# Attention scores of a masked graph network: 4 matmuls of 32x128 or 16 matmuls of 32x32 per key tile

## The chip, the cores and the metric

The kernel runs on one core of a Trainium2 chip. The metric is the device time of one execution in microseconds. Before the change it was 3508.07 us, the median of three runs (3501.76 to 3508.48).

## The reference

Two layers work on x of 16 batches x 1024 nodes x 256 features, with a 0/1 adjacency matrix of 1024 x 1024 per batch. Each layer takes `h = relu(layernorm(x))` and adds its result to x. The change lies in the first layer, which is masked self-attention of 8 heads of 32 features, followed by an MLP:

```python
normed = layer_norm(h, gamma1, beta1)
qkv = normed.reshape(b, n, 8, 32).transpose(0, 2, 1, 3)
scores = einsum('bhqd,bhkd->bhqk', qkv, qkv) / sqrt(32)
attn = softmax(where(adj > 0, scores, -inf), axis=-1)
out = einsum('bhqk,bhkd->bhqd', attn, qkv)
x1 = h + out
layer0 = x1 + gelu(layer_norm(x1, gamma2, beta2) @ W1 + b1) @ W2 + b2
```

Queries, keys and values are the same array. The second layer is a graph attention of one head with weights `leaky_relu(Ax^T + Ay + h a_12 h^T)`, masked by the same adjacency, softmax, a product with the features, two projections and an `elu`. All arithmetic on TensorE is in f32, apart from the masks of batch 0, which are fp8.

## The kernel before

Two paths are in the program. A bound on gamma and beta chooses the fast one, `fast_path`, which is the only one that runs here; everything below is about it.

**Tiling of the first layer's attention.** The 1024 nodes are 8 tiles of 128 (`P`). Queries go in two halves of 512 (`QW`), heads in two groups of 4 (`GH`, `NG`). `kT[r, g, :]` holds the transposed normed features: partitions are the 4 x 32 features of the 4 heads of group `g`, so head `j` lies in partitions 32j to 32j+31 (`r`). For each unit (query half, head group, key tile), `scores` in line 950 makes, for each of the 4 heads, the product of 128 keys (the stationary operand, 32 partitions x 128 columns) and 512 queries (the moving operand, 32 partitions x 512 columns). The result of a head is 128 x 512 f32 in PSUM, one bank. The four heads use four row strips of the array, and each its own bank: heads 0 and 1 write `sc[0]`, heads 2 and 3 `sc[1]`, two buffers of one slot each (pool `psc`, `bufs=1`).

VectorE then adds the mask to a buffer of two heads (line 971), ScalarE takes the exponential (line 974), and in the turn after it `weigh` multiplies by the values (line 987): per head a matmul with 128 rows x 32 columns of stationary operand, the four heads in four column strips of the array, into the four partition quarters of one accumulator `o`. In batch 0 the mask of the first two heads is added by TensorE ahead of the scores, with an fp8 identity as stationary operand (`by_pe`), and the scores accumulate on it. The exponentials of the eight key tiles are summed by DMAs that GpSimd issues (line 1011).

**Quarters.** All other large matmuls go through the helper `matmul` in line 565, which splits a 128-column stationary operand into four matmuls of 32 columns (line 570), one for each column strip, as long as `quarters[0]` holds. It is switched off when the attention of the last batch closes. Transposes use the whole array.

**Order.** The program is written as six generators, which are merged by due places: `stream_a` runs the attention of batch b, and `stream_b` at the same time the rest of batch b-1 (MLP, then the second layer), in pieces of about 1.75 us of TensorE work. So TensorE's instruction order is: a score unit of one key tile, line 987 for the unit before, some pieces of the other stream, the next score unit. There are 16 x 2 x 2 x 8 = 512 score units. Within an engine the order of the program is kept.

**Shapes on the array.** In records of the profile, "32*128" is the shape of the stationary operand (rows * columns). So TensorE meets 32*128 for scores, 128*32 for line 987 and the helper's quarters, 128*128 for transposes.

Of the kernel before, what the change touches and what calls it, by code (L numbers as in the profile page):

```python
# [16 lines left out]
P = 128  # L17
# [476 lines left out]
def fast_path(  # L494
# [28 lines left out]
    nc = tc.nc  # L523
    B, N, D = x.shape
    DFF = W1.shape[1]
    H, HD = 8, D // 8
# [38 lines left out]
    def matmul(out, lhsT, rhs, start=True, stop=True):  # L565
        if not quarters[0]:
            nc.tensor.matmul(out, lhsT, rhs, start=start, stop=stop)  # L567
            return
        for c in range(0, P, HD):
            nc.tensor.matmul(out[c : c + HD], lhsT[:, c : c + HD], rhs, start=start, stop=stop)  # L570
# [165 lines left out]
    def defer(us, f):  # L736
        deferred.append((clock[0] + us, len(deferred), f))

        return clock[0] + us
# [145 lines left out]
    def make_turns():  # L885
        room = 3 - open_sums[0] - bool(summed) if open_sums[0] else 100
        while turns and turns[0][0] <= room:
            n, f = turns.pop(0)
            room -= n
            f()  # L890
# [40 lines left out]
    def attention(b, st):  # L931
        va, kT = st["va"], st["kT"]


        def scores(qh, g, kt):
            qs = slice(qh * QW, (qh + 1) * QW)
            sc = [
                psc.tile([P, 2, QW], F32, tag=f"sc{i}", name=f"s_{b}_{g}_{qh}_{kt}_{i}") for i in range(2)
            ]

            by_pe = 2 if b == 0 else 0
            if by_pe:
                for j in range(by_pe):
                    matmul(
                        sc[j // 2][:, j % 2, :], ident8, st[qh][:, kt // 2, :, kt % 2], start=True, stop=False
                    )
                clock[0] += 0.45
            for j in range(GH):
                r = slice(j * HD, (j + 1) * HD)
                nc.tensor.matmul(  # L950
                    sc[j // 2][:, j % 2, :],
                    kT[r, g, kt * P : (kt + 1) * P],
                    kT[r, g, qs],
                    start=j >= by_pe,
                    stop=True,
                )
            mb = st[qh][:, kt // 2, :, kt % 2].unsqueeze(1).to_broadcast([P, 2, QW])
            es = []
            if b == 0 and kt % 2:

                odd = midp.tile([P, 2, 2, QW], F32, tag="mid", name=f"odd_{g}_{qh}_{kt}")
            for i in range(2):
                if b == 0 and kt % 2:
                    e = odd[:, i]
                elif kt == 0:
                    e = accp.tile([P, 2, QW], F32, tag=f"acc{i}", name=f"acc_{b}_{g}_{qh}_{i}")
                else:
                    e = ep.tile([P, 2, QW], F32, tag="e", name=f"e_{b}_{g}_{qh}_{kt}_{i}")
                masked = sc[i]
                if 2 * i >= by_pe:  # L970
                    nc.vector.tensor_tensor(e, masked, mb, op=ALU.add)  # L971
                    masked = e
                es.append(e)
                weights = lambda e=e, masked=masked: nc.scalar.activation(e, masked, AF.Exp, scale=SCALE)  # L974
                if i == 0:
                    weights()
            return es, weights

        acc = {}


        def weigh(qh, g, kt, es):
            if kt == 0:
                acc[g, qh] = pso.tile([P, QW], F32, tag="o", name=f"o_{b}_{g}_{qh}")
            o = acc[g, qh]
            for j in range(GH):
                nc.tensor.matmul(  # L987
                    o[j * HD : (j + 1) * HD, :],
                    va[:, kt, (g * GH + j) * HD : (g * GH + j + 1) * HD],
                    es[j // 2][:, j % 2, :],  # L990
                    start=(kt == 0),
                    stop=(kt == NT - 1),
                )
            if b == 0 and kt % 2:

                if kt > 1:
                    for n, (e, w) in enumerate(zip(es, odds[g, qh])):
                        defer(1.0 + 2.5 * n, lambda e=e, w=w: nc.vector.tensor_add(e, e, w))
                odds[g, qh] = es
            if kt == NT - 1:  # L1000
                c = tmpp.tile([P, QW], F32, tag="w2", bufs=3, name=f"os_{b}_{g}_{qh}")
                nc.vector.tensor_copy(c, o)
                weighed.append((b, qh, g, c, [s[g, qh] for s in (sums, odds) if s]))

        sums, odds = {}, {}


        def add_up(qh, g, kt, e, i):
            if b == 0 and kt % 2:
                return  # L1010
            nc.gpsimd.dma_start(sums[g, qh][i], e, accum_op=ALU.add)  # L1011

        units = [(qh, g, kt) for qh in range(NQH) for g in range(NG) for kt in range(NT)]
        for u in units:
            make_turns()
            es, rest_of_weights = scores(*u)
            go_on()
            rest_of_weights()
            qh, g, kt = u
            if kt == 0:  # L1020
                sums[g, qh] = es
            else:
                for i in range(2):
                    defer(2.0 + 1.5 * i, lambda u=u, e=es[i], i=i: add_up(*u, e, i))
            scored.append((weigh, (*u, es)))
            yield

    def go_on():
        was_weighed, was_summed, was_totalled = weighed[:], summed[:], totalled[:]
        for l in (weighed, summed, totalled):  # L1030
            l.clear()
        if scored:
            f, args = scored.pop()
            f(*args)
        summed.extend(was_weighed)
        for args in was_summed:
            total(*args)
        for args in was_totalled:
            turns.append((2, lambda args=args: finish(*args)))
        clock[0] += 2.0  # L1040
# [501 lines left out]
```

## Time and profile before

| | before |
|---|---|
| median of 3 runs | 3508.07 us |
| the profiled execution | 3501.46 us |
| its span, first to last instruction | 3499.6 us |
| granted TensorE clock, mean | 0.998 |
| line 987, weights times values: busy, mean of one record | 461.8 us, 605 ns |
| line 971, masks added on VectorE: busy, mean | 1002.6 us, 1217 ns |
| line 974, exponentials on ScalarE: busy, mean | 896.0 us, 1057 ns |
| fillers of line 570, 256 columns: mean of one record | 379 ns |

How to read it. A line of the profile has the source line, engine, operation, the tiles written and read, the shape of the stationary operand, the moving operand and the count. Then come the busy time in us and the mean of one record in ns, then the engine's idle time ahead of them and what ended most of it. Busy time is the union of the records, so overlapping records count once. TensorE appears twice, as PE (matmuls) and as PEld (loads of the stationary operand). An f32 matmul is two LDWEIGHTS records and two MATMUL records, for two passes over the moving operand. The ends of matmul records are modelled, their starts are not, so distances between starts say more than durations.

### The profile page before, as it was taken

What the parts mean: (1) busy time and instruction counts of PE and PEld (TensorE: products, weight loads), DVE (VectorE), ACT (ScalarE), POOL (GpSimd) and SP (SyncE); (2) the same over time, 40 slices, a digit from 0 to 9 for tenths busy, and PEclk for the clock granted to TensorE, in tenths of its full rate; (3) what the DMA queues carried; (4) which work ended last, traced back from release to release, by engine and by line L of the source; (5) the groups of instructions that cost most, each with busy time, mean ns of one, the idle gap of its engine ahead of it and who ended that gap; (6) DMA issues with size and microseconds to landing.
All of it is one profiled execution on the core that took longest, in us unless ns stands there. A gap on an engine that the chain in (4) does not pass through costs nothing.

```text
span 3499.6 us, 107320 instructions
## 1 busy us (share of the span) xinstructions
PE 3445.0 (98%) x46590; PEld 1673.9 (48%) x46590; DVE 2758.3 (79%) x5193; ACT 1857.8 (53%) x2184; POOL 1412.8 (40%) x1708
## 2 busy tenths in 40 slices
PE   6999999999999999999999999999999999999998
PEld 2244444444444444444444444444444444444477
DVE  6878788787877878888787888878878777887754
ACT  4555555555555555555555555555555555555522
POOL 3444443434434344343444534344344443434220
PEclk9999999999999999999999999999999999999999
DMA  7798889999899998989989899998989989899720
GB/s 183 147 182 173 181 164 185 182 186 188 161 187 176 191 184 165 181 167 190 195 167 183 165 185 185 177 190 164 186 177 191 183 165 179 171 191 182 147 63 14
DMA packets 281860, 597.81 MB, mean 171 GB/s; under 512 B 94882, under 2 KB 130084, under 8 KB 281380
## 3 DMA queue, kind: packets, MB, share of 16 engines
q0 software_dynamic: 124416, 453.04, 70.1%
q1 hardware_dynamic: 154276, 134.41, 15.5%
q8 instruction: 368, 6.03, 0.7%
q10 hardware_dynamic: 2688, 3.41, 0.3%
q14 instruction: 112, 0.92, 0.1%
HBM read 104.21 MB, written 16.78 MB: 35 GB/s over the span
## 4 chain that ended last, share of the span: by engine, by line
PE 94%; DVE 3%; DMA 1%; issue 1%; ACT 0%; POOL 0%; ACTq 0%; SPq 0%; DVEq 0%; POOLq 0%
PE s L950 15%; PE o L987 13%; PE pa L570 12%; PE po L570 12%; PE ph L570 12%; PE lg L570 10%; PE pg L570 3%; PE pf L570 3%; PE puT L570 3%; PE den L901 2%; PE ptf L1193 1%; PE pty L1117 1%; PE ptk L801 1%; PE ptos L922 1%; PE pa L567 1%
## 5 line engine op out<-in xcount | busy, mean ns | idle before, releaser
L974 ACT ACTIVATE e<-e 128x1024 f32<-128x1024 f32 x852 | 896.0, 1057 | 964.3 <-DVE e L971 728.3
L1011 POOL DMA_DIRECT2D acc<-e x864 | 754.9, 890 | 1438.3 <-DMA acc<-e 637.3
L971 DVE TENSOR_TENSOR e<-s,mk 128x1024 f32<-128x1024 f32 x852 | 1002.6, 1217 | 181.2 <-PE s L950 155.4
L950 PE MATMUL s<-kT 32*128 32x512 f32 x4096 | 592.5, 643 | 3.5 <-DVE odd L971 2.7
L987 PE MATMUL o<-e,va 128*32 128x512 f32 x3456 | 461.8, 605 | 2.1 <-ACT e L974 2.1
L570 PE MATMUL pa<-gw,e 128*32 128x258 f32 x7648 | 453.0, 380 | 0.0
L570 PE MATMUL lg<-fT,uT 128*32 128x256 f32 x7680 | 447.3, 379 | 0.0
L570 PE MATMUL ph<-yT,w 128*32 128x256 f32 x7808 | 446.5, 379 | 0.0
L570 PE MATMUL po<-w,hid 128*32 128x256 f32 x7680 | 439.3, 379 | 0.0
L570 PEld LDWEIGHTS ph<-yT,w 128*32 128x32 f32 x7808 | 255.3, 110 | 211.8 <-issue 51.1
L570 PEld LDWEIGHTS po<-w,hid 128*32 128x32 f32 x7680 | 250.3, 110 | 208.8 <-issue 58.3
L570 PEld LDWEIGHTS pa<-gw,e 128*32 128x32 f32 x7648 | 248.4, 110 | 212.0 <-issue 56.5
L570 PEld LDWEIGHTS lg<-fT,uT 128*32 128x32 f32 x7680 | 249.6, 110 | 209.0 <-issue 43.4
L1241 DVE SCALAR_TENSOR_TENSOR e<-lg,gw,mk 128x256 f32<-128x256 f32 x512 | 223.2, 477 | 72.0 <-PE lg L570 61.5
L1247 ACT ACTIVATE e<-e,shift 128x512 f32<-128x512 f32 x256 | 183.1, 717 | 181.6 <-DVE e L1246 116.0
L1144 DVE TENSOR_TENSOR hid<-ph,b1c 128x512 f32<-128x512 f32 x256 | 175.8, 687 | 91.6 <-PE ph L570 80.1
L950 PEld LDWEIGHTS s<-kT 32*128 32x128 f32 x4096 | 162.7, 184 | 163.8 <-issue 112.0
L987 PEld LDWEIGHTS o<-e,va 128*32 128x32 f32 x3456 | 68.6, 108 | 330.3 <-issue 187.3
L974 ACT ACTIVATE acc<-acc 128x1024 f32<-128x1024 f32 x124 | 131.1, 1057 | 132.9 <-DVE acc L971 128.4
L1246 DVE SCALAR_TENSOR_TENSOR e<-e 128x512 f32<-128x512 f32 x256 | 193.1, 754 | 8.8
L971 DVE TENSOR_TENSOR acc<-s,mk 128x1024 f32<-128x1024 f32 x124 | 146.1, 1218 | 20.2 <-PE s L950 19.8
L793 POOL TENSOR_TENSOR nrm<-nrm,g 128x256 f32<-128x256 f32 x128 | 112.9, 882 | 63.8 <-DVE nrm L727 63.8
(145 smaller groups left out, 3820.9 us busy)
## 6 DMA issues: line engine op xcount, KB each, us to landing
acc<-e POOLq DMA_DIRECT2D x864, 512.0 KB, 6.1
adj<-in_adj_dram SPq DMA_DIRECT2D x248, 256.0 KB, 5.6
h<-in_x_dram SPq DMA_DIRECT2D x64, 256.0 KB, 6.1
xb<-in_x_dram SPq DMA_DIRECT2D x128, 128.0 KB, 4.3
out_dram<-z SPq DMA_DIRECT2D x128, 128.0 KB, 4.0
adj<-in_adj_dram SPq DMA_DIRECT2D x4, 512.0 KB, 6.8
mk<-mq SPq DMA_TRANSPOSE x128, 6.5
w<-in_L_gnn_W_dram ACTq DMA_DIRECT2D x2, 1024.0 KB
```

What stands on the lines that cost most here:

```text
L570: nc.tensor.matmul(out[c : c + HD], lhsT[:, c : c + HD], rhs, start=start, stop=stop)
L793: nc.gpsimd.tensor_mul(nrm, nrm, g1)
L901: nc.tensor.matmul(den[j * HD : (j + 1) * HD, :], ones, acc[j // 2][:, j % 2, :], start=acc is accs[0], stop=acc is accs[-1],)
L950: nc.tensor.matmul(sc[j // 2][:, j % 2, :], kT[r, g, kt * P : (kt + 1) * P], kT[r, g, qs], start=j >= by_pe, stop=True,)
L971: nc.vector.tensor_tensor(e, masked, mb, op=ALU.add)
L974: weights = lambda e=e, masked=masked: nc.scalar.activation(e, masked, AF.Exp, scale=SCALE)
L987: nc.tensor.matmul(o[j * HD : (j + 1) * HD, :], va[:, kt, (g * GH + j) * HD : (g * GH + j + 1) * HD], es[j // 2][:, j % 2, :], start=(kt = ...
L1011: nc.gpsimd.dma_start(sums[g, qh][i], e, accum_op=ALU.add)
L1144: nc.vector.tensor_tensor(hid[:, f0 : f0 + 2, :], ph, b1c[:, f0 : f0 + 2].unsqueeze(2).to_broadcast([P, 2, CW]), op=ALU.add,)
L1241: nc.vector.scalar_tensor_tensor(e[:, j, :], lg[:, j, :], gw[:, kt, D : D + 1], st[c // 2][:, kt // 2, qs, kt % 2], op0=ALU.add, op1=ALU.add,)
L1246: nc.vector.scalar_tensor_tensor(e, e, ALPHA, e, op0=ALU.mult, op1=ALU.max)
L1247: ready = defer(2.5, lambda: nc.scalar.activation(e, e, AF.Exp, bias=shift))
```

## The change

Each head's 128 keys are cut into four quarters of 32. A score matmul then has a stationary operand of 32 x 32 and writes 32 partitions of the head's bank; one unit has 16 of them, one for each combination of row strip (head) and column strip (key quarter). The order is head by head, and within a head quarter by quarter. The first matmul of a buffer in each quarter starts or continues the sum as before (`start=j >= by_pe`). Nothing else is touched.

```diff
             for j in range(GH):
                 r = slice(j * HD, (j + 1) * HD)
-                nc.tensor.matmul(
-                    sc[j // 2][:, j % 2, :],
-                    kT[r, g, kt * P : (kt + 1) * P],
-                    kT[r, g, qs],
-                    start=j >= by_pe,
-                    stop=True,
-                )
+                for c in range(0, P, HD):
+                    nc.tensor.matmul(
+                        sc[j // 2][c : c + HD, j % 2, :],
+                        kT[r, g, kt * P + c : kt * P + c + HD],
+                        kT[r, g, qs],
+                        start=j >= by_pe,
+                        stop=True,
+                    )
             mb = st[qh][:, kt // 2, :, kt % 2].unsqueeze(1).to_broadcast([P, 2, QW])
```

Lines after 950 stand one line lower in the changed kernel: its score matmuls are in line 951, weights times values in line 988.

## The prediction

> **What bounds the kernel now.** I read the page first, its parts 1 and 4, then the costliest groups, to learn which engine sets the end and what share of it the changed line holds.
>
> ```profile
> span 3499.6 us, 107320 instructions
> ...
> PE 3445.0 (98%) x46590; PEld 1673.9 (48%) x46590; DVE 2758.3 (79%) x5193; ACT 1857.8 (53%) x2184; POOL 1412.8 (40%) x1708
> ...
> PE 94%; DVE 3%; DMA 1%; issue 1%; ACT 0%; POOL 0%; ACTq 0%; SPq 0%; DVEq 0%; POOLq 0%
> ...
> L950 PE MATMUL s<-kT 32*128 32x512 f32 x4096 | 592.5, 643 | 3.5 <-DVE odd L971 2.7
> ```
>
> TensorE is busy in 98% of the span, and the chain that ended last runs through it for 94%. The changed line was kept waiting by others for 3.5 us in all. So the change is worth what it adds to or takes from TensorE's own time, 512 times: 16 batches x 2 query halves x 2 head groups x 8 key tiles. The 4096 records are 512 units of 8: each f32 matmul leaves two MATMUL records and two LDWEIGHTS records, two passes.
>
> Next the chain in order of time, for the cost of a unit on the path rather than its busy time, which holds modelled pipeline ends:
>
> ```profile
> 1999.85 0.87 PE pa L570 x16
> 2000.72 1.07 PE s L950 x8
> 2001.79 1.00 PE o L987 x8
> 2002.79 1.73 PE lg L570 x32
> ```
>
> One score unit holds the path for 1.07 us. Then the two lines' own instructions, with least, median and longest duration in ns:
>
> ```profile
> L950 PEld LDWEIGHTS s<-kT x4096: 181/184/333, 25.9 to 3334.7; 32*128 32x128 f32 x196
> L950 PE MATMUL s<-kT x4096: 587/692/1218, 25.9 to 3335.1; 32*128 32x512 f32 x196
> L987 PEld LDWEIGHTS o<-e,va x3456: 105/109/110, 43.3 to 3341.7; 128*32 128x32 f32 x192
> L987 PE MATMUL o<-e,va x3456: 592/593/618, 43.3 to 3342.1; 128*32 128x512 f32 x192
> ```
>
> A score's second pass lasts 587 and its first 692: 105 ns in which the first waits for its own 128 weight columns. In line 987, with 32 columns, the same difference is 618 - 592, some 26 ns. And last the timeline of TensorE in four slices of 4 to 7 ns at the start of one unit, then the one burst of tiny matmuls that the program has:
>
> ```profile
> 1988.13 0.69 PE L950 MATMUL s<-kT 32*128 32x512 f32 x1
> 1988.13 0.70 PE L950 MATMUL s<-kT 32*128 32x512 f32 x2
> 1988.13 0.71 PE L950 MATMUL s<-kT 32*128 32x512 f32 x3
> 1988.13 0.71 PE L950 MATMUL s<-kT 32*128 32x512 f32 x4
> ```
>
> ```profile
> 72.72 0.31 PE L570 MATMUL p_w_a<-a2c,stage 128*32 128x1 f32 x16 [0.65 <-ACT wm L689]
> 73.00 0.43 PE L570 MATMUL p_w_a<-a1c,stage 128*32 128x1 f32 x32
> ```
>
> The four heads of a unit start one after the other, 6.7 ns apart. The masks of batch 0 (fp8, one pass, two records per matmul) start 3.4 ns apart in the trace, so a tile's place in line costs 1.67 ns for each of its records, and four for an f32 matmul. A tile's second pass does not hold up the next tile: all four first passes start within 20 ns, the four second passes together 533 ns later. From the last second-pass start of a unit to the first weight load of line 987 are 516 ns in all 512 units.
>
> So the 1.07 us are: 105 (load of 128 columns, in the open) + 20 (three further starts) + 2 x 427 (two passes of 512 columns, as in 1.73 us for eight passes of 256) + 89 [...] = 1068.
>
> [...] 93 to 95 ns between the end of streaming and the first load at every change of shape, 88 to 89 when leaving 32x128, whichever shapes meet. [...]
>
> **The change, part by part.** Order on DVE, ACT, POOL and SP stays the same instruction for instruction, as do waits and DMAs. On TensorE, each of the 2048 score matmuls becomes four: 48 more records per unit, 24,576 in all, same arithmetic.
>
> *Removed:* the load of 128 columns becomes one of 32 in the open: 105 - 26 = 79 ns less[...]. 512 x 80 = 41.0 us less.
>
> *Added:* 16 starts in place of 4. Twelve more x 6.7 ns = 80 ns before the last tile begins; it still has its two passes to run, so its delay is the unit's. 512 x 80 = 41.0 us more. Bounds: [...] if the starts were wholly hidden, 0. Above, the sixteen f32 tiles need 64 records at once, and the densest 64 in this trace are the 32 matmuls (with 32 loads) of p_w_a, started from 73.00 to 73.26, 0.27 us or 4.2 ns per record. At that pace 15 tiles x 4 x 4.2 = 252 ns, 232 more than now: 119 us. [...] I take 6.7.
>
> *Kept:* two passes of 427 (the heads still write four banks, and four column tiles already stream the same rows in line 987); both changes of shape, since neighbours are 128x32 or 128x128 before and after.
>
> *Waits and queues:* the wait for the second score buffer now stands before eight tiles in place of two, and behind it line 987 and the filler pieces; line 950 waited 3.5 us in total for DVE, so nothing is added. The first buffer is complete at 27 + 7 x 6.7 + 854 = 928 ns, against 105 + 7 + 854 = 966; the second at 27 + 100 + 854 = 981 against 979. DVE, which waits for scores but does not set the end, sees no difference. Instruction fetch grows by 24,576 x 64 B = 1.6 MB on 6.03 + 0.92 MB, beside 597.81 MB moved; hidden.
>
> *Sum:* -41 + 41 (+2 ns of rounding per unit, 1 us) = about +1 us on the profiled execution: span 3499.6 to about 3500.6, execution 3501.46 to 3502.5. The median of the runs shown is 3508.07, 6.6 above the profiled one; on that scale 3509.
>
> **Rivals.** (1) *The sixteen starts are cheaper than four records each*, or part of them hides behind the loads: [...] against it, 6.7 in the trace with this type. Gain 20 to 41 us: 3467 to 3488, centre 3478.
>
> (2) [...] A unit asks for 64 records within 107 ns. [...] if only half are there and the rest come at p_w_a's 4.2 ns, the last tile starts at about 134 + 27 ns, 34 ns late, 17 us; if none, 119 - 41 = 78 us. It decides from about 14 ns per unit (7 us). For it: no burst of this density in the profile besides p_w_a's. Against: 48 matmuls of p_w_a start within 0.55 us, the second burst without a slower end. 3525 to 3587, centre 3556.
>
> (3) *The sequencer's mean pace binds.* Now 46,590 matmul records in 3445 us are 74 ns each; then 58,878, which is 58.5. [...] Fillers of 256 columns already run at 54 ns per record (1.73 us / 32), but over 64 records at most[...]; against it stands p_w_a.
>
> (4) *It does not do what it says:* tiles of one row group cannot run beside the others; then a unit takes four turns, 3 x 854 ns more, 512 x 2.56 = 1312 us: 4820.
>
> **How the numbers follow.** Balance as computed 0.44, own range 3503 to 3519 (6.7 to 8 ns per tile); rival 1 0.22; rival 2 0.20; rival 3 0.09; rival 4 0.05. About 0.2%, 7 us, is what a measurement of this kernel tells from no change; of the 0.44, 0.38 falls within it, 0.04 above, 0.02 below. Faster 0.02 + 0.22 = 0.24, same 0.38, slower 0.04 + 0.20 + 0.09 + 0.05 = 0.38. The range takes in rivals 1 and nearly all of 2: 3466 to 3580, leaving out about 0.17.
>
> **What would show it.** Of the changed kernel: 16384 score records less the few missing; first passes about 26 ns longer than second ones, not 105; the sixteenth start about 100 ns after the first; a unit of 1.07 us in the chain. A unit near 0.99 means that the starts were hidden (rival 1); 1.10 to 1.22 with a widening gap between starts, rival 2; fillers slower than 1.73 us per 32, rival 3; 3.6 us per unit, rival 4. Any change in line 987 or the fillers' own time makes my sum wrong, since I have left them as they are.

## The result: 0.33% slower, most of it one step after the scores

The changed kernel took 3515.98 us (median of 20 runs, 3508.09 to 3526.79), the kernel before 3504.98 us (20 runs, 3499.36 to 3512.45). The ratio is 1.0033, with a 95% interval of 1.0024 to 1.0042. The profiled execution's span grew by 9.4 us.

From the page of the changed kernel: span, busy time of the engines, chain by engine, the group of score matmuls.

```profile
span 3509.0 us, 131896 instructions
...
PE 3452.0 (98%) x58878; PEld 1785.2 (51%) x58878; DVE 2754.0 (78%) x5193; ACT 1858.4 (53%) x2184; POOL 1423.3 (41%) x1708
...
PE 93%; DVE 3%; DMA 2%; issue 1%; ACT 0%; POOL 0%; ACTq 0%; SPq 0%; DVEq 0%; POOLq 0%
...
L951 PE MATMUL s<-kT 32*32 32x512 f32 x16384 | 591.1, 602 | 4.8 <-DVE odd L972 4.6
```

TensorE still sets the end, with the 12,288 further matmul records. Its score group is not busier, 591.1 us against 592.5. Now the score line's own instructions (least, median, longest ns) and the same stretch of the chain in order of time:

```profile
L951 PEld LDWEIGHTS s<-kT x16384: 101/104/150, 26.3 to 3343.4; 32*32 32x32 f32 x200
L951 PE MATMUL s<-kT x16384: 587/609/1058, 26.3 to 3343.8; 32*32 32x512 f32 x200
```

```profile
2003.99 1.75 PE pa L570 x32
2005.74 1.07 PE s L951 x32
2006.81 1.01 PE o L988 x8
2007.82 1.73 PE lg L570 x32
```

The unit is 1.07 us as before. What is longer stands in the next line: 1.01 in place of 1.00 for line 988 (line 987 before). This is a digit of two places, so I looked at the four strips' starts. Four slices of 2 ns of the changed kernel's TensorE timeline, at 2, 16, 24 and 44 ns after the first start:

```profile
2006.74 0.62 PE L988 MATMUL o<-e,va 128*32 128x512 f32 x1
2006.74 0.62 PE L988 MATMUL o<-e,va 128*32 128x512 f32 x2
2006.74 0.64 PE L988 MATMUL o<-e,va 128*32 128x512 f32 x3
2006.74 0.65 PE L988 MATMUL o<-e,va 128*32 128x512 f32 x4
```

And of the kernel before, at 2, 16 and 24 ns:

```profile
2001.72 0.62 PE L987 MATMUL o<-e,va 128*32 128x512 f32 x1
2001.72 0.63 PE L987 MATMUL o<-e,va 128*32 128x512 f32 x3
2001.72 0.64 PE L987 MATMUL o<-e,va 128*32 128x512 f32 x4
```

The count at the end says how many matmuls of line 988 (987 before) have begun. Before, three strips ran after 16 ns and all four after 24. Now it is two and three, and the fourth comes only later. Over all 512 units the median starts were 0, 7, 13, 20 ns before and are 0, 7, 22, 38 ns now. The fillers that follow keep this skew: the fourth strip's first filler starts 36 ns after the first strip's by the median, and 20 ns before the change. It is paid at the next change of shape: after a filler of 256 columns, the next unit starts some 309 ns after the fourth strip's last matmul has begun, in both kernels. From one score unit to the next the changed kernel falls behind the kernel before by a median of 16.0 ns; over 511 steps that is 8.2 us, of 8.3 us that it falls behind from the first unit to the last. The other 1.1 us of the span lie ahead of the first unit (0.4) and after the start of the last (0.7). So about three quarters of the 11.0 us between the medians are explained by line 988.

### The profile page after: what moved, and what is told of

Same layout as the page of the kernel before. It is cut to its first block, busy times and chain, and to the rows that moved or that the text cites. A ratio compares the mean times of both kernels' runs of the same rounds, so it can differ in the third digit from the quotient of the medians.

```text
span 3509.0 us, 131896 instructions
## 1 busy us (share of the span) xinstructions
PE 3452.0 (98%) x58878; PEld 1785.2 (51%) x58878; DVE 2754.0 (78%) x5193; ACT 1858.4 (53%) x2184; POOL 1423.3 (41%) x1708
## 4 chain that ended last, share of the span: by engine, by line
PE 93%; DVE 3%; DMA 2%; issue 1%; ACT 0%; POOL 0%; ACTq 0%; SPq 0%; DVEq 0%; POOLq 0%
PE s L951 15%; PE o L988 14%; PE pa L570 12%; PE ph L570 12%; PE po L570 11%; PE lg L570 10%; PE pf L570 3%; PE pg L570 3%; PE puT L570 3%; PE den L901 2%; DMA acc<-e 1%; PE pty L1118 1%; PE ptf L1194 1%; PE ptk L801 1%; PE pa L567 1%
## 5 line engine op out<-in xcount | busy, mean ns | idle before, releaser
L951 PE MATMUL s<-kT 32*32 32x512 f32 x16384 | 591.1, 602 | 4.8 <-DVE odd L972 4.6
L988 PE MATMUL o<-e,va 128*32 128x512 f32 x3456 | 468.9, 604 | 2.1 <-ACT e L975 2.1
L570 PEld LDWEIGHTS ph<-yT,w 128*32 128x32 f32 x7808 | 286.4, 110 | 180.9 <-issue 48.8
L570 PEld LDWEIGHTS pa<-gw,e 128*32 128x32 f32 x7648 | 281.1, 110 | 179.4 <-issue 53.3
L570 PEld LDWEIGHTS po<-w,hid 128*32 128x32 f32 x7680 | 281.7, 110 | 177.3 <-issue 54.7
L570 PEld LDWEIGHTS lg<-fT,uT 128*32 128x32 f32 x7680 | 280.6, 110 | 178.4 <-issue 41.3
L988 PEld LDWEIGHTS o<-e,va 128*32 128x32 f32 x3456 | 75.7, 108 | 364.8 <-issue 212.2
L951 PEld LDWEIGHTS s<-kT 32*32 32x32 f32 x16384 | 120.1, 103 | 164.7 <-issue 111.5
```

Source lines behind the costliest of these rows:

```text
L951: nc.tensor.matmul(sc[j // 2][c : c + HD, j % 2, :], kT[r, g, kt * P + c : kt * P + c + HD], kT[r, g, qs], start=j >= by_pe, stop=True,)
L988: nc.tensor.matmul(o[j * HD : (j + 1) * HD, :], va[:, kt, (g * GH + j) * HD : (g * GH + j + 1) * HD], es[j // 2][:, j % 2, :], start=(kt = ...
```

## The experiments

My theory (A) is about a count: once there are some 64 records whose matmuls have not ended, what comes next in order starts late, and a record counts until its matmul has ended. The 64 is an estimate from two kernels: with 16 records in a score unit line 987 was in time, and with 64, which sixteen f32 tiles have, the third and fourth strips of line 988 are 9 and 18 ns late. By this count 48 records in a unit would leave room for the 16 of line 988. That a record counts until its matmul has ended was a guess. The late strips start 15 and 16 ns after the one before, some 4 ns for each of a matmul's four records, close to the 4.2 of the densest burst in the prediction. What in TensorE makes such a limit no trace here shows. Rivals: each further record costs a little wherever it stands (B); the 32x32 shape, or the order in which strips come free, makes line 988 late (C); a record ceases to count before its matmul ends, so that a second half only waits for the first half in its own tile (D).

**Keys in halves, 8 tiles of 32x64.**

```diff
-                for c in range(0, P, HD):
+                for c in range(0, P, 64):
...
-                        sc[j // 2][c : c + HD, j % 2, :],
-                        kT[r, g, kt * P + c : kt * P + c + HD],
+                        sc[j // 2][c : c + 64, j % 2, :],
+                        kT[r, g, kt * P + c : kt * P + c + 64],
```

> Keys in two halves: 8 score matmuls of 32x64 per unit, 32 records in place of 16 (before) or 64 (after). Theory A [...]: 32 records leave room, so line 988's four strips start at 0, 7, 13, 20 ns as before. The unit is 53 (load of 64 columns) + 47 (seven further starts) + 854 + 89 = 1043 ns, 27 less than before; 512 x 27 = 14 us: ratio to before 0.996, about 3491 us. Theory B (each further record on TensorE costs 11 us / 24,576 = 0.45 ns wherever it stands): 8192 more records cost 3.7 us, less 14 us: ratio 0.997. Theory C (it is the new shape of the array that costs, whatever its records): line 988's strips start late as in the changed kernel, 0, 7, 22, 38 ns; -14 + 9 us, ratio 0.9985.

Measured: 3492.4 us, ratio 0.9963 (0.9951 to 0.9975), faster than both kernels. Strips of line 988 at 0, 7, 13, 20 ns, unit 1044 ns, median step -27.0 ns per unit. In the profile of this kernel, the score instructions and the same stretch of the chain:

```profile
L951 PEld LDWEIGHTS s<-kT x8192: 127/131/227, 25.4 to 3327.3; 32*64 32x64 f32 x200
L951 PE MATMUL s<-kT x8192: 587/638/1112, 25.4 to 3327.7; 32*64 32x512 f32 x200
```

```profile
1998.67 1.04 PE s L951 x16
1999.71 1.00 PE o L988 x8
2000.71 1.73 PE lg L570 x32
```

The first passes are 638 - 587 = 51 ns longer than the second: the load of 64 columns. With the starts (seven more, 47 ns) it is a shorter way in than 4 tiles (105 + 20) or 16 (25 + 100). This run speaks for A against C in the wider sense, that any cutting of the columns makes line 988 late; its ratio can't tell A from B. The step can: B's 0.45 ns for each of 16 further records would have left -20 ns in place of -27.

**The loops exchanged, key quarter outside.**

```diff
-            for j in range(GH):
-                r = slice(j * HD, (j + 1) * HD)
-                for c in range(0, P, HD):
+            for c in range(0, P, HD):
+                for j in range(GH):
+                    r = slice(j * HD, (j + 1) * HD)
```

> The changed kernel with the two loops exchanged: key quarter outside, head inside, so the last four tiles of a unit are the four row strips of one column strip. Theory A: the same 64 records, nothing changes: line 988's strips start at 0, 7, 22, 38 ns, ratio to before 1.003. Theory C (the strips of line 988 start late because the column strips 2 and 3 of the array are released late by the last score tiles): the pattern of starts changes, since now strip 3 ends 27 ns after strip 2, and strips 0 and 1 are free 50 ns earlier; then 0, 7, 27, 50 or so. Theory B: ratio 1.003.

Measured: ratio 1.0052 (1.0033 to 1.0070). The strips start at 0, 7, 22, 38 ns again and the median step is 16.0 ns, so the order of release is not the cause: C's pattern did not appear. The total was higher than I expected, which the repetition below takes up.

**Eight tiles twice, 64 records of which half end early.** The edit is to the kernel before; its removed lines are not shown.

```diff
+            for q in range(0, QW, 256):
+                for j in range(GH):
...
+                    for c in range(0, P, 64):
...
+                            sc[j // 2][c : c + 64, j % 2, q : q + 256],
+                            kT[r, g, kt * P + c : kt * P + c + 64],
+                            kT[r, g, qh * QW + q : qh * QW + q + 256],
+                            start=j >= by_pe,
+                            stop=q > 0 or j >= by_pe,
```

> Keys in two halves and queries in two: all eight 32x64 tiles for the first 256 queries, then all eight for the other 256. 64 records per unit as in the changed kernel, but the first 32 end in the middle of the unit. Theory A: [...] line 988 is there in time and its strips start at 0, 7, 13, 20 ns. The unit is 53 + 47 + 4 passes of 216 + 89 = 1053 ns, 17 less than before: -9 us, ratio 0.9975. Theory B (by number of records): -9 + 11 us, ratio 1.0006, line 988 late by 17 ns per unit.

Measured: strips at 0, 7, 13, 20 ns, unit 1049 ns, median step -22.0 ns. A slice of its timeline, 24 ns after the first start (the line has number 989 here):

```profile
1999.48 0.64 PE L989 MATMUL o<-e,va 128*32 128x512 f32 x4
```

All four strips have begun, where the changed kernel had three. With as many records as there, the line is in time. This rules out B, and the starts are just what A says. The ratio, 0.9992 (0.9983 to 1.0001), is worse than the 0.9975 of A: -11 us of steady steps should have come, and about 3 did. The difference lies outside the steady steps, in single waits, of which more below.

**Sixteen tiles twice, 128 records.** The same edit with quarters in place of halves.

> Sixteen 32x32 tiles for the first 256 queries, then sixteen for the other 256: 128 records per unit[...]. Theory A: records 65 to 128 can come only as the first tiles end, from some 0.6 us on, one per some 4 ns; the last tile starts its second half at about 0.87 us instead of 0.55, and the unit takes about 1.4 us in place of 1.07: 512 x 0.35 = +180 us, ratio 1.05. Theory B (0.45 ns per record): 73,728 more records than before are 33 us, ratio 1.009. Theory D [...]: the second halves queue behind the first in each tile, the unit is 1.08 us, ratio about 1.004.

Measured: 3680.45 us, ratio 1.0499 (1.0478 to 1.0520). The stretch of the chain of waits in this kernel:

```profile
1993.69 1.42 PE s L952 x60
1995.12 1.00 PE o L989 x8
1996.11 3.45 PE po L570 x64
```

The unit is 1.42 us, the median step +354 ns. By the medians of all units, tiles 1 to 16 begin within 101 ns. One tile's second half begins at 456 ns, directly after its first, and no other until 649 ns. From there a further one starts about every 16.7 ns until 883 ns, and the second passes follow at the same spacing until 1120 ns. The weight loads show the gap, first the whole unit, then the stretch from 378 to 628 ns after its start, in which only one load runs:

```profile
1993.62 1.01 PEld L952 LDWEIGHTS s<-kT 32*32 32x32 f32 x64 [0.17 <-DVE xb L1173]
1994.08 0.10 PEld L952 LDWEIGHTS s<-kT 32*32 32x32 f32 x1
```

So seventeen f32 matmuls, 68 records, had begun when the pause came. The eighteenth began some 196 ns after the first tile's last pass stopped streaming (240 + 213 = 453, an estimate with half of the 427 ns that 512 columns take), and from there the pace was 16.7 / 4 = 4.2 ns per record.

These two figures also give the changed kernel's starts. There the first tile's last pass stops streaming at 453 + 427 = 880 ns after the unit's start. Line 988 begins with the seventeenth matmul, and the seventeenth was not held up in the run with 128 records (456 ns, directly after its tile's first half); the eighteenth to twentieth would come at 880 + 196 = 1076, at 1093 and at 1109 ns. Measured, the four strips start at 1071, 1078, 1093 and 1109 ns.

D's 1.004 and B's 1.009 are far off. Here too line 989 starts at 0, 7, 13, 20, with 32x32 tiles before it. I put this down to the late tiles, which start 16.7 ns apart and so end apart; no run varied this.

**Twelve tiles, 48 records.** Head 3's scores are left out; the mask is added to head 2's in their place.

```diff
-            for j in range(GH):
+            for j in range(GH - 1):
...
-                masked = sc[i]
+                masked = sc[i] if i == 0 else sc[i][:, 0:1, :].to_broadcast([P, 2, QW])
```

> The changed kernel with the scores of head 3 of each group left out (the mask is added to head 2's instead), so 12 tiles of 32x32 and 48 records per unit, same shapes, same work on the other engines. Theory A [...] its strips start at 0, 7, 13, 20 ns. The unit is 27 + 11 x 6.7 + 854 + 89 = 1044 ns, 27 less than before: -14 us, ratio to before 0.996. Theory C (a score unit of 32x32 shape makes line 988 late): starts 0, 7, 22, 38 as in the changed kernel, -27 + 16 ns per unit, -6 us, ratio 0.9984.

Measured: strips at 0, 7, 13, 20 ns, unit 1044 ns, median step -27.0 ns, all as A has them. Again 24 ns after the first start:

```profile
2001.81 0.64 PE L988 MATMUL o<-e,va 128*32 128x512 f32 x4
```

C in its last form, the 32x32 shape, is out. But the time was slower than before: ratio 1.0023 (1.0009 to 1.0037). At the last unit this execution is 20 us behind the kernel before, though its steady steps put it 13.8 us ahead. Some 34 us are therefore in single waits, which A does not speak of.

**The changed kernel and the exchanged loops, again side by side.**

> The changed kernel itself once more, on the same chip as the next run. Theory A: 16 ns per unit more than before, ratio 1.0024 to 1.004.

> The exchanged loops once more, since its ratio of 1.0052 in four runs lay above the changed kernel's 1.0033. Theory A: the loops' order costs nothing in itself, ratio within 0.1% of the run beside it; its first profile had 10 us of single delays in batch 0. If the order does cost, the ratio stays at about 1.005.

Measured: 1.0042 (1.0028 to 1.0056) and 1.0058 (1.0044 to 1.0072), both with a median step of 16.0 ns. The first lies just above its expectation of 1.0024 to 1.004. The second expectation, equal within 0.1%, was missed by 0.06%, with intervals that overlap. The loops' order does not change the step; whether it adds single waits stays undecided.

**What makes twelve tiles slow.** Six tiles of 32x64 with the same head left out, and the two earlier kernels once more beside it on one chip.

```diff
-                for c in range(0, P, HD):
+                for c in range(0, P, 64):
```

> Six tiles of 32x64: keys in halves, head 3's scores left out as in the run with 12 tiles (head 2's are used in its place). That run had the unit and the starts of theory A, but its time was 1.0023 of before, some 22 us above what they give. This one has the same leaving out with 24 records per unit. If the leaving out itself (VectorE reads one bank twice) brings the 22 us, it comes here too: unit 53 + 5 x 6.7 + 854 + 89 = 1030 ns, -20 + 22 us, ratio about 1.0005. If the 22 us come with the number of records (48 against 32), ratio 0.994.

> Keys in two halves once more, beside the 12 tiles on one chip: their score unit and line 988 take the same time. 0.996 as before; if it was the chip or the hour that made the 12 tiles slow, this one comes out near 1.002 too.

> The 12 tiles once more, beside the halves: near 1.002 again if it is its own, near 0.996 if it was the chip.

Measured: six tiles 0.9974 (0.9960 to 0.9987), unit 1031 ns, median step -40.0 ns; halves 0.9972 (0.9965 to 0.9979); twelve tiles 1.0027 (1.0015 to 1.0039). So it was neither chip nor hour. Six tiles came between my two expectations: its 14.0 us of single waits, against 3.4 and 6.9 for the halves, took back the further 6.6 us that its steps gain over them. Where such waits are, in the second profile of twelve tiles, from TensorE's table of waits (us in total, times, longest):

```profile
PE den L901 <- DMA acc<-e: 6.1, 5, 3.2
```

and in its TensorE timeline one of those, and another kind:

```profile
1186.78 0.62 PE L901 MATMUL den<-acc,ones 128*32 128x512 f32 x2 [3.19 <-DMA acc<-e]
...
1187.23 1.00 PE L901 MATMUL den<-acc,ones 128*32 128x512 f32 x2
```

```profile
1638.06 1.07 PE L951 MATMUL s<-kT 32*32 32x512 f32 x13
1639.82 1.07 PE L951 MATMUL s<-kT 32*32 32x512 f32 x11 [0.69 <-issue]
```

The first is the end of a head group: line 901 sums the exponentials that GpSimd's DMAs have added up, and they landed 3.19 us late (before, this wait was 1.9 us in the whole kernel, its longest 1.4). After some of these pauses TensorE ran at half clock for 3.4 or 6.8 us; the mean granted clock was 0.994 in this execution and 0.998 before. Leaving out the last 30 us, the stretches at half clock add up to 34.1 us in each of the two profiles of twelve tiles and to 10.2 us before, so at half speed they account for up to 12 of the 33 us (an estimate).

The second is a unit cut in two, 13 and 11 records, by a pause in which TensorE waited for nothing that its semaphores show. Packets of one DMA queue stand near such pauses: q8, which the page calls "instruction". In the changed kernel it had 464 packets and 7.60 MB, before 368 and 6.03 MB: 16 KB per packet, and 64 B for each of the 24,576 further records. After the first 160 us, the two profiles of twelve tiles have eight units with such a cut inside a score buffer, three of them at the same record in both. Each goes on 1.3 to 1.6 us after a packet of this queue has landed; here it landed at 1638.50, and the unit went on at 1639.82. That the packets are the cause was not shown: no run varied them. Why 48 records of 32x32 get more of all this than 32 records of 32x64 with the same step stays open.

For all kernels, steady steps (median step x 511) and the rest of the lag at the last unit, from one profiled execution each:

```
kernel            records  step ns  steps us  rest us  ratio
changed                64    +16.0      +8.2     +0.1  1.0033
changed, again         64    +16.0      +8.2    +14.9  1.0042
loops exchanged        64    +16.0      +8.2    +11.7  1.0052
  again                64    +16.0      +8.2    +10.4  1.0058
16 tiles twice        128   +354.0    +180.9     -1.6  1.0499
8 tiles twice          64    -22.0     -11.2     +7.5  0.9992
keys in halves         32    -27.0     -13.8     +6.9  0.9963
  again                32    -27.0     -13.8     +3.4  0.9972
12 tiles               48    -27.0     -13.8    +33.9  1.0023
  again                48    -27.0     -13.8    +33.3  1.0027
6 tiles                24    -40.0     -20.4    +14.0  0.9974
```

The step is the same to the nanosecond in every repetition; the rest is not. It is probably what spreads the 20 runs of the changed kernel over 19 us, though runs without a profile can't be split in this way.

## Why the prediction was right, and where it was off

The forecast of 3509 us was 7 us low; 3516 lies in its range and in the likeliest case's own range of 3503 to 3519. That it lies in the latter is in part luck. That range stood for starts of 6.7 to 8 ns; the starts came at 6.7, and most of the excess came from line 988, which the sum put at nothing. The forecast was also 3 us higher for resting on a median of three runs of the kernel before: against the 20 runs, about +1 us was forecast and +11.0 measured. No change and slower had been given 0.38 each; it is 0.33% slower, by none of the rivals' paths.

- *Removed, the load of 128 columns:* right. First passes last 612 and second ones 587 ns by their medians (the line's 609 is the median of both together): 25 ns, where it was 105, so 80 less.
- *Added, twelve further starts at 6.7 ns:* right. The sixteenth tile starts 100 ns after the first, so rival 1 is out. That starts could be cheaper than 6.7 ns, with the 20 us at the low end of its gain, was not shown by any trace.
- *Their sum, zero for the score unit:* right, 1071 ns before and after.
- *Kept, passes and changes of shape:* right. Entering 32x32 costs 94 to 95 ns and leaving it 89, as with 32x128; the sixteen tiles run at once, so rival 4 is out. The 516 ns from a unit's last second pass to the first load of line 987 held, to within 1 ns, in 508 of the 512 units before, not in all.
- *Rival 3, the sequencer's mean pace:* out. It needed a least mean pace of more than 58.5 ns per matmul record, which no trace here shows. Fillers still take 1.73 us per 32, 54 ns each, and the late matmuls of the run with 128 records, two MATMUL records each, start 16.7 ns apart. The trace of before already spoke against it more than I said: fillers ran at 54 ns per record over 96 records in a row (5.18 us), not over 64 at most.
- *Waits and queues:* this step failed. I named line 987 as queued behind the scores and put its cost at nothing, because the wait in front of line 950 is short. It was not a semaphore that kept it: the matmuls of line 988 waited 2.1 us for one in the whole changed kernel, as those of line 987 did before. Its strips are late with 64 records ahead of them (0, 7, 22, 38 ns), and not with 48 (0, 7, 13, 20). The term is +16 ns x 512 = 8.2 us instead of 0. The prediction did name the sign by which this shows, a change in line 987 or in the fillers.
- *Rival 2* had the 4.2 ns per record right, and the place wrong: it put the delay inside the score unit, 34 ns if half of the records were there. The unit's own starts stay 6.7 ns apart over all 64 records; late are the third and fourth strips of the line after it, by 9 and 18 ns.

That records of ended matmuls no longer count agrees with the pair of 64-record kernels (0, 7, 22, 38 against 0, 7, 13, 20), with the 128 records, which pause after the 68th, and with the starts at 1076, 1093 and 1109 ns that follow from these. If A holds, the count does not fall record by record as passes end: in the run with 128 records all sixteen first passes had stopped streaming by 341 ns (101 + 27 + 213, an estimate), so with the same 196 ns the eighteenth matmul would have begun by 537 ns, yet it began at 649. Whether the count falls in program order or a whole matmul at a time, whether it is of records or of f32 matmuls, and what in TensorE stands behind it, no run here separates. The last 1.7 us between the steady steps with lead and tail (9.3 us) and the medians' 11.0 are not traced; single waits, which differ from one execution to the next, can hold them.

## What to carry to other kernels

Cutting matmuls into array tiles had three prices in these traces: the load in the open (105, 51 and 25 ns for 128, 64 and 32 columns), the starts (6.7 ns for each further f32 tile), and the delay of the line after them (18 ns for its fourth strip with 64 records ahead of it that had not ended, none with 32 or 48). Find the cut where load and starts together are least, here 32x64 (51 + 47 ns, against 105 + 20 and 25 + 100), and then look whether the next line still starts in time: here it did with 48 records ahead of its own 16. When a step is priced at nothing because its wait is short, look at its starts too: the late strips of line 988 show in no semaphore wait.

## What the runs showed that I had not expected

- A strip that started late stayed late. Of the 18 ns that the fourth strip lost at line 988, 16 were still there in the fillers (36 ns after the first strip, against 20), and were paid when the shape changed: 16.0 ns from one score unit to the next.
- In this kernel, in which TensorE is busy for 98% of the span, a faster steady step did not reach the end whole: of 13.8 us for the halves 10 to 13 came through, of 20.4 us for the six tiles 9. The waits for the DMA sums in line 901 were 1.9 us in total before, and 2.6 to 3.7 in these three profiles, which is only a part of what was lost.
